# Mamba block and mixture of experts on one Trainium2 core: the last expert tiles in one run of pairs, begun on their own weights, with three partial sums in place of five

## The chip, the cores and the metric

The kernel runs on one core of a Trainium2 chip. The metric is the device time of one execution in microseconds. A core has TensorE (PE in the profile, its weight loads PEld), VectorE (DVE), ScalarE (ACT), GpSimd (POOL) and SyncE (SP, which here only issues transfers); each runs its own instructions in the order in which the program emits them and waits on semaphores. Sixteen DMA engines move the data that all queues ask for.

## What is computed

The input x has 4096 rows of 256 numbers, float32 throughout. Cut to what matters, with `ln` a layer norm over a row:

```python
# selective scan block (256 -> 512 inner channels, 16 states a channel)
x_in, z = split(x @ W_in.T)
u  = silu(causal_conv(x_in, 4 taps) + b_conv)
dt = softplus(u @ W_dt.T + b_dt);  B = u @ W_B.T;  C = u @ W_C.T
h[t] = exp(dt[t] * A) * h[t-1] + dt[t] * B[t] * u[t]      # per channel and state
y[t] = sum over states of h[t] * C[t]
x1 = ln(x + (y * silu(z)) @ W_out.T)
# mixture of 32 experts, 6 a row, and one shared expert
p = softmax(x1 @ router.T);  chosen = top6(p + bias);  w = p[chosen] / sum
out = ln(x1 + shared(x1) + sum over chosen e of w[e] * down[e](silu(gate[e](x1)) * up[e](x1)))
```

## The kernel before, in words

**Chunks and units.** The 4096 rows are cut into nine chunks: 256 rows, seven of 512, 256 (`SIZES`, NC = 9). The outer loop is the scan: 512 units, each one `tensor_tensor_scan` of 128 x 512 (L1236) on VectorE and one product with C (L1243). A full chunk has 64 units, the first and the last (numbers 0 and 8) have 32. Around a unit, `du_at` makes dt*u*B on POOL four units ahead (L1100), `exp_at` the decay on ACT two units ahead (L1111), `load_bc` fetches the broadcast rows of B and C by SP (bb and cb), and `summed` adds the product into PSUM by four TensorE transposes, three units late (L1157).

**Order by generators.** All else is written as Python generators in the list `threads`. `step()` advances each of them to its next `yield`; one such pass is called a round here. Nothing runs in Python on the chip: the rounds only set where each instruction stands in its engine's order. A unit of a full chunk emits one round, a unit of chunk 0 or 8 two, and behind the scan rounds follow without units. `rounds(k)` waits k rounds, `room()` waits for one of the PSUM banks (three while the scan runs, eight after it), `take` and `give` count live buffers.

**Beside chunk c** run `front(c + 1)` (projection, convolution, step sizes; its `gate(c)` makes z), `tail(c - 1)` (out-projection, norm, then `prepare`: router, top 6, places of the rows, shared expert), and tiles of chunk c - 2. With six units left, `drain(*mains)` steps until `front` and `tail` are through. `tail` adds the out-projection from PSUM to `row`, the chunk's rows of x (L1040; `row` has one buffer), two rounds after its matmuls (L1031). `prepare` reads the router's logits from PSUM one round after their matmuls (L317, L323). It starts `copies`, which scatters each row to its six places in `xs` by indirect DMAs of POOL, one a round (L553; `apart_from` asks that another POOL operation lies between two of them), and it writes the lists of rows and experts to DRAM (`order`). At its end it stores x1 plus the shared expert's part into the first partial sum, `acc[0]` (`base`, one buffer, L402 and L406).

**Tiles.** The scattered rows fill 224 tiles of 128 rows with one expert each, handled in 112 pairs. `loaded` issues a pair's transfers by SP: its rows (xt, L611) and weights of rows (wt, L613) and, for a tile with weights of its own, the expert's gu (256 KB, L622) and dn (128 KB, L627). `tiles` walks the pairs: it loads pair i, then begins pair i - `AHEAD`, with `gap` rounds between two begun. `pair` transposes the rows (L638, copied by ACT at L641), multiplies by gu (L679), applies the gate on ACT (tanh, L687) and VectorE (L690), multiplies by dn (L697) and scales on ACT (L655); `added` then adds each tile's 128 rows to a partial sum in DRAM by an accumulating indirect DMA of POOL (L661). `pair_of` does the same on the **wall**, a tile of all 32 experts' weights that stays in SBUF (L1285, tanh L1292, L1294 and L1295, transposes L1301, L1311).

**The wall's place** is that of the scan's operands: `cut` lays taps, W_dt, scratch, the inputs of the convolution, u, dt, the transposed x, W_in, z and W_out into it one after another, and `READY` notes up to which expert a place is free at four moments: at the start of chunk 8 (18 experts), when z of chunk 8 is made (22), when the scan is over (27), when the last out-projection has been emitted (32). `walls` issues the experts' loads in that order (L796, L800), one in three rounds while the scan runs.

**The end.** Tiles of chunks 1 to 6 (62 pairs) run on weights of their own beside the scan, into `acc[0]` to `acc[2]`. Then the program steps until the last out-projection and those tiles are emitted, and only then do the remaining 50 pairs (12 of chunk 7, 38 of chunk 8) begin, all on the wall, after `stored`, into `acc[2]` to `acc[4]`. Beside them `halfway` adds up `acc[0]` and `acc[1]` in SBUF (L1327 to L1330). When all is emitted, `finish` runs eight times on 512 rows: three loads of 512 KB (L1338), an add on POOL (L1340), two on VectorE (L1342, L1344), the norm (L179 to L193) and the store (L1347). A chunk's tiles can be loaded when its copies are all emitted (`copied`).

## Time and profile before

| what | value |
|---|---|
| runs of the kernel before | median 1891.46 us of 3 (1890.25 to 1893.32) |
| the profiled execution, its own time | 1901.56 us |
| its span, first to last instruction | 1899.9 us |
| busy in the span: PE, DVE, ACT, POOL | 72%, 75%, 56%, 64% |
| first scan L1236, last scan | 50.3 us, 1581.9 us |
| starts of the chunks 1 to 8 | 156, 323, 493, 669, 857, 1051, 1245, 1432 us |
| first wall group L1285, last | 1608.4 us, 1818.5 us |
| last accumulating DMA of POOL issued | 1835.15 us |

A row of the profile gives an operation with its line, its count, and the mean time of one. A window row gives each engine's busy time in a stretch with the number of instructions, the clock that TensorE was granted, the share of time that the DMA engines were busy, and GB/s. A row of waits says what an engine's instruction stood waiting for: total, times, longest. "issue" stands for time in which an engine waited for nothing that the profile shows.

### The profile page before, as it was taken

What the parts mean: (1) busy time and instruction counts of PE and PEld (TensorE: products, weight loads), DVE (VectorE), ACT (ScalarE), POOL (GpSimd) and SP (SyncE); (2) the same over time, 40 slices, a digit from 0 to 9 for tenths busy, and PEclk for the clock granted to TensorE, in tenths of its full rate; (3) what the DMA queues carried; (4) which work ended last, traced back from release to release, by engine and by line L of the source; (5) the groups of instructions that cost most, each with busy time, mean ns of one, the idle gap of its engine ahead of it and who ended that gap; (6) DMA issues with size and microseconds to landing.
All of it is one profiled execution on the core that took longest, in us unless ns stands there. A gap on an engine that the chain in (4) does not pass through costs nothing. (4 is left out here: it accounts for less than half of the span.)

```text
span 1899.9 us, 24943 instructions
## 1 busy us (share of the span) xinstructions
PE 1359.1 (72%) x6354; PEld 969.4 (51%) x6354; DVE 1430.4 (75%) x2435; ACT 1057.2 (56%) x2400; POOL 1220.2 (64%) x961
## 2 busy tenths in 40 slices
PE   6768665965786597868877896778766665799930
PEld 5335343633553365555556564666554544677720
DVE  2579899899889988997889788989986744233227
ACT  5586464555465456655666475647556442355523
POOL 1335555457556746895689667966895674677763
PEclk8777785987789689978988898789887787899965
DMA  8228975535744686988778887878878997699977
GB/s 247 80 83 285 277 227 169 158 97 164 226 133 116 173 241 195 220 206 238 209 201 216 225 229 182 220 218 247 210 192 228 276 257 193 113 202 210 168 150 264
DMA packets 349359, 377.22 MB, mean 199 GB/s; under 512 B 66816, under 2 KB 284480, under 8 KB 349216
## 3 DMA queue, kind: packets, MB, share of 16 engines
q1 hardware_dynamic: 305632, 317.78, 58.2%
q0 software_dynamic: 41472, 57.80, 16.1%
q8 instruction: 52, 0.85, 0.2%
q14 instruction: 91, 0.75, 0.1%
q10 hardware_dynamic: 2112, 0.05, 0.1%
HBM read 258.08 MB, written 117.43 MB: 198 GB/s over the span
## 5 line engine op out<-in xcount | busy, mean ns | idle before, releaser
L1100 POOL TENSOR_TENSOR du<-wall,bb 128x512 f32<-128x512 f32 x512 | 698.9, 1420 | 423.1 <-DVE h L1236 237.8
L1236 DVE TENSOR_TENSOR_SCAN h<-h,hlast,du 128x512 f32<-128x512 f32 x512 | 657.0, 1283 | 35.4 <-ACT h L1128 21.4
L1157 PE MATMUL y<-ident,hc 128*128 128x128 f32 x2048 | 362.5, 316 | 158.2 <-DVE hc L1243 148.8
L1157 PEld LDWEIGHTS y<-ident,hc 128*128 128x128 f32 x2048 | 282.2, 164 | 261.6 <-DVE hc L1243 194.6
L1243 DVE TENSOR_TENSOR hc<-h,cb 128x512 f32<-128x512 f32 x512 | 354.1, 692 | 59.7 <-DMA cb<-bcd 22.1
L1111 ACT ACTIVATE h<-wall,aneg 128x512 f32<-128x512 f32 (+1 forms) x576 | 371.0, 644 | 40.0 <-DVE hc L1243 21.5
L553 POOL DMA_INDIRECT xs<-row,at x192 | 192.3, 1002 | 95.2 <-DVE at L476 33.5
L661 POOL DMA_INDIRECT acc<-yt,no x124 | 196.8, 1587 | 66.3 <-ACT yt L655 31.5
L1138 ACT COPY hlast<-h 128x1 f32<-128x1 f32 x448 | 70.8, 158 | 256.4 <-DVE hc L1243 253.2
L661 POOL DMA_INDIRECT acc<-ytl,no x100 | 157.0, 1570 | 52.0 <-ACT ytl L655 19.9
L930 PE MATMUL pd<-wall 128*128 128x512 f32 (+1 forms) x288 | 127.4, 590 | 48.4 <-DVE hm L691 42.2
L679 PE MATMUL pg<-xsT,gu 128*128 128x128 f32 x992 | 135.3, 295 | 14.3 <-ACT hlast L1138 12.1
L679 PEld LDWEIGHTS pg<-xsT,gu 128*128 128x128 f32 x992 | 132.1, 211 | 21.5 <-ACT hlast L1138 12.8
L894 PE MATMUL pv<-wall 128*128 128x512 f32 (+1 forms) x288 | 120.5, 563 | 2.6 <-ACT hlast L1136 1.6
L697 PE MATMUL po<-dn,hm 128*128 128x256 f32 x248 | 79.2, 449 | 54.0 <-issue 33.4
L930 PEld LDWEIGHTS pd<-wall 128*128 128x128 f32 x288 | 57.2, 207 | 101.9 <-issue 90.8
L1285 PE MATMUL pg<-wall,xsT 128*128 x400 | 101.5, 400 | 0.0
L1294 DVE SCALAR_TENSOR_TENSOR gt<-gt,pg 128x256 f32<-128x256 f32 x50 | 21.0, 420 | 106.2 <-ACT gt L1292 82.4
L638 PE MATMUL pt<-ident,xt 128*128 128x128 f32 x448 | 72.6, 284 | 39.2 <-issue 18.3
L697 PEld LDWEIGHTS po<-dn,hm 128*128 128x128 f32 x248 | 50.5, 220 | 76.8 <-issue 41.3
L638 PEld LDWEIGHTS pt<-ident,xt 128*128 128x128 f32 x448 | 55.9, 146 | 63.2 <-issue 38.2
L641 ACT COPY xsT<-pt 128x512 f32<-128x512 f32 x112 | 65.5, 584 | 36.6 <-PE pt L638 28.4
(198 smaller groups left out, 2042.4 us busy)
## 6 DMA issues: line engine op xcount, KB each, us to landing
bb<-bcd SPq DMA_DIRECT2D x256, 256.0 KB
cb<-bcd SPq DMA_DIRECT2D x256, 256.0 KB
xs<-blank SPq DMA_DIRECT2D x55, 578.0 KB
gu<-in_gate_up_t_dram SPq DMA_DIRECT2D x124, 256.0 KB
xt<-xs SPq DMA_DIRECT2D x224, 128.5 KB
acc<-blank SPq DMA_DIRECT2D x32, 512.0 KB
dn<-in_down_t_dram SPq DMA_DIRECT2D x124, 128.0 KB
wall<-acc SPq DMA_DIRECT2D x24, 512.0 KB
```

The lines of the kernel that those rows point to most:

```text
L553: i = nc.gpsimd.indirect_dma_start(out=xs, out_offset=bass.IndirectOffsetOnAxis(ap=at[:, b, k : k + 1], axis=0), in_=row[:, b, :], in_offs ...
L638: nc.tensor.transpose(pt4[:, i, k, :], xt[:, i, ts(k, P)], ident)
L661: a = nc.gpsimd.indirect_dma_start(out=acc[lane + (j + i) % TURN], out_offset=bass.IndirectOffsetOnAxis(ap=no[:, i : i + 1], axis=0), in_= ...
L679: nc.tensor.matmul(pg[:, h, i, :], gu[i][:, k, ts(h, P)], xT[:, i, k, :], start=(k == 0), stop=(k == KD - 1),)
L697: nc.tensor.matmul(po[:, i, :], hm[:, i, :], dn[i], start=True, stop=True)
L894: nc.tensor.matmul(pv, taps[:, m, k, :], xin[:, m, k : k + Tc], start=(k == 0), stop=(k == TAPS - 1),)
L930: nc.tensor.matmul(pd, w_dt[:, k, ts(m, P)], u[:, k, :], start=(k == 0), stop=(k == M - 1),)
L1100: nc.gpsimd.tensor_mul(parts(q, du), u, row_for(q, 0))
L1111: nc.scalar.activation(h[:, ts(i, Tc)], dt_of[c][:, m + i, :], AF.Exp, scale=aneg[:, m + i, n : n + 1],)
L1157: nc.tensor.matmul(y_of[c, g][b // 2][:, b % 2, ts(m + j - 2 * g, P)], hc[:, ts(j * nb + b, P)], ident, start=(opens and j == 0 and b % 2 ...
L1236: nc.vector.tensor_tensor_scan(h, h, du_of.pop(q), hlast[:, n, m : m + 1], ALU.mult, ALU.add)
L1243: nc.vector.tensor_mul(parts(q, hc), parts(q, h), row_for(q, 1))
```

## The change

The tiles of chunks 6, 7 and 8 become one list, walked by one `tiles` from the start of chunk 8 to the end: 12 pairs of chunk 6 and the first 12 tiles (`EARLY`, six pairs) of chunk 7 on weights of their own, the other 44 pairs on the wall once it is stored. The program no longer steps until the earlier tiles are emitted; the scan's pools are closed right after its last product. Pairs on their own weights are begun one load behind (`AHEAD` 1 in place of 2), pairs on the wall two as before; a pair's load waits until three rounds after the matmuls on the buffer that it takes. u and dt of chunk 8, which are half as long, take the half of their places that lies next to the other, and z the second half of its place, so that other experts are free at the four moments (19, 5, 4 and 4 in that order). All tiles add into three partial sums; `halfway` and its sums are gone. The rows of chunk 8 have a tile of their own, loaded before the scan. `tail` waits three rounds in place of two before it reads PSUM (but not for chunk 8), `prepare` two in place of one. In chunk 8 only `last_gate` is drained. The copies of chunk 7 no longer wait for another POOL operation in between.

```diff
-    LANES = 5
-    TURN = 3
-    AHEAD = 2
+    LANES = 3
+    AHEAD = 1, 2
+    EARLY = 12
...
     def step():
+        clock[0] += 1
         threads[:] = [g for g in threads if alive(g)]
...
# prepare, between the router's matmuls and the maximum
         yield
+        yield
         mx = stat.tile([P, NB], F32, tag="mx", name=f"mx_{c}")[:, :nb]
...
# copies
-                while apart_from[0] and c < NC - 1:
+                while apart_from[0] and c < NC - 2:
                     yield
...
# added
-                out=acc[lane + (j + i) % TURN],
+                out=acc[(j + i) % LANES],
...
# pair, behind the matmuls on gu
         give("xsT")
+        used_at[j] = clock[0]
...
-    def tiles(items, gap, weights, one):
+    def tiles(items):
         st, going, begun = {}, [], [0]
+        def gap():
+            return 3 if scanned else 4
         def begin(upto):
             while begun[0] < upto:
                 k = begun[0]
                 begun[0] += 1
+                one = pair if items[k][2] else pair_of[0]
                 going.append(one(items[k][1], *st.pop(k)))
                 threads.append(going[-1])
-                yield from rounds(gap)
+                yield from rounds(gap())
-        for i, (c, j) in enumerate(items):
+        for i, (c, j, own) in enumerate(items):
+            weights = qw if own else None
+            ahead = AHEAD[not own]
+            if not own and not stored:
+                yield from begin(i)
+                while not stored:
+                    yield
             if c not in copied:
                 yield from begin(i)
                 while c not in copied:
                     yield
                 if c >= NC - 2:
                     yield from rounds(4)
             if weights is not None:
                 yield from take("dn", 4)
+                while i > 2 and clock[0] < used_at.get(items[i - 3][1], clock[0]) + 3:
+                    yield
             while i > 2 and items[i - 3][1] not in turned_out:
                 yield
             st[i] = loaded(c, j, weights)
-            yield from begin(i + 1 - AHEAD)
+            yield from begin(i + 1 - ahead)
...
# the places in the wall: cut(shape, moments at which its equal parts come free)
-    us[odd], dts[odd] = cut(M, T), cut(M, T)
-    z_all = cut(NB, DI)
+    us[odd], dts[odd] = cut((M, T), 0, 2), cut((M, T), 2, 0)
+    w_in = cut((KD, 2 * DI), 1)
+    xTs[odd] = cut((KD, T), 1)
+    z_all = cut((NB, DI), 1, 3)
+    w_out = cut((M, D), 3)
...
# walls: experts sorted by the latest moment that any part of their place needs
+        for e in sorted(range(E), key=lambda e: stages[e]):
+            while not free_at[stages[e]]():
+                yield
...
# front and gate, chunk 8
-            u = us[c % 2][:, :, :Tc]
+            u = us[c % 2][:, :, :Tc] if c < NC - 1 else half_of(us[c % 2], 1)
-            dt = dts[c % 2][:, :, :Tc]
+            dt = dts[c % 2][:, :, :Tc] if c < NC - 1 else half_of(dts[c % 2], 0)
-            z = z_all[:, : blocks(c)]
+            z = z_all[:, : blocks(c)] if c < NC - 1 else z_all[:, NB - blocks(c) :]
...
# tail
-                yield
-                yield
+                yield from rounds(3 if c < NC - 1 else 2)
                 part = row[:, 2 * h : 2 * h + 2, :D]
...
# before the scan
+        row_of[NC - 1] = const.tile([P, blocks(NC - 1), RW], F32, tag="row_last", name="row_last")
+        load_rows(NC - 1)
...
# in the scan
                 if 2 <= c:
-                    late = tiles(stage(c - 2), 4, qw, pair)
-                    threads.append(late)
+                    items = stage(c - 2)
+                    if c == NC - 1:
+                        items += stage(c - 1, 0, EARLY) + stage(c - 1, EARLY, own=False)
+                        items += stage(c, own=False)
+                    rest = tiles(items)
+                    threads.append(rest)
...
             if left[c] == 6:
-                drain(*mains)
+                drain(*mains[c == NC - 1 :])
...
# behind the scan
         last_tail = tail(NC - 1)
         threads.append(last_tail)
-        while NC - 1 not in z_done or late in threads:
-            step()
...
# finish
-        for i in range(TURN):
-            nc.sync.dma_start(part[:, i], rows_of(acc[LANES - TURN + i], b, MANY))
+        for i in range(LANES):
+            nc.sync.dma_start(part[:, i], rows_of(acc[i], b, MANY))
         yield
         nc.gpsimd.tensor_add(part[:, 0], part[:, 0], part[:, 1])
-        whole = sums[:, b : b + MANY, :]
-        nc.vector.tensor_add(whole, whole, part[:, 2])
         yield
-        nc.vector.tensor_add(whole, whole, part[:, 0])
+        whole = part[:, 0]
+        nc.vector.tensor_add(whole, whole, part[:, 2])
```

## The prediction

> **What bounds the kernel now.** I read the table of windows first, cut at the scan's chunks (the starts of L1236) and at what follows its end.
>
> ```profile
> core 0: us, PE busy (x) PEld busy (x) DVE busy (x) ACT busy (x) POOL busy (x), PEclk, DMA share, GB/s
> ...
> 1245.00:1432.00 187.00, 137.16 (x762) 112.26 (x762) 164.75 (x273) 108.51 (x256) 143.56 (x115) 0.84 0.82 219
> 1432.00:1583.00 151.00, 97.59 (x534) 79.92 (x534) 97.24 (x190) 76.56 (x205) 96.84 (x77) 0.79 0.95 254
> 1583.00:1605.00 22.00, 10.15 (x40) 7.91 (x40) 7.29 (x32) 6.13 (x11) 6.10 (x5) 0.66 0.75 212
> 1605.00:1640.00 35.00, 22.34 (x88) 17.52 (x88) 11.25 (x56) 6.94 (x19) 18.83 (x23) 0.74 0.61 115
> 1640.00:1820.00 180.00, 164.74 (x836) 131.60 (x836) 51.17 (x113) 99.84 (x278) 136.67 (x87) 0.97 0.91 175
> 1820.00:1840.00 20.00, 1.57 (x6) 0.88 (x6) 0.18 (x1) 3.22 (x6) 13.96 (x10) 0.59 0.64 84
> 1840.00:1900.00 60.00, 0.00 (x0) 0.00 (x0) 43.37 (x104) 18.13 (x40) 20.71 (x8) 0.50 0.84 274
> ```
>
> Six stages with six limits. A full chunk of the scan (row one) is VectorE's: 165 of 187 us. The last chunk (1432 to 1583) is not: its 32 units take 4.7 us each, where a scan and its product are 1.28 + 0.69; no engine is above two thirds, but the DMA share is 0.95. Then comes a hole of 22 us, in which the last out-projection and ten experts' weights are fetched; a slow start of 35 us; 180 us in which TensorE and POOL are both nearly full; 20 us of POOL alone; 60 us of VectorE and DMA. Next the waits in the last chunk and the timeline of POOL at the end of the tiles:
>
> ```profile
> DVE gt L690 <- ACT gt L687: 21.1, 6, 7.0
> ...
> DVE base L402 <- DMA acc<-base: 12.3, 1, 12.3
> ...
> DVE row L1040 <- DMA row<-in_x_dram: 9.6, 1, 9.6
> ```
> ```profile
> 1829.60 1.54 POOL L661 DMA_INDIRECT acc<-ytl,no  x1 [0.31 <-issue]
> 1831.45 1.55 POOL L661 DMA_INDIRECT acc<-ytl,no  x1 [0.30 <-issue]
> 1833.30 1.55 POOL L661 DMA_INDIRECT acc<-ytl,no  x1 [0.30 <-issue]
> ```
>
> The last chunk's scan stands behind tile products whose weights have not come (first row). And POOL's adds follow each other every 1.855 us, so a pair of tiles costs POOL 3.71 us; TensorE's cost for a wall pair is 3.62 us (starts of its group L1285 in the steady part: 1653.27, 1656.88, 1660.50). From 1654 on 92 adds take 183 us, of which 171 are this step and 12 are gaps: **POOL's queue, not TensorE, sets the end of the tiles**, at 1835.15 + 1.55 and 2.4 of landing, 1839.
>
> **The change, part by part**, against the profiled execution: span 1899.9, its own time 1901.56, 10.1 above the median 1891.46 of the runs. I sum in span and take 8.4 off at the end (1899.9 - 1891.46).
>
> *Chunks 0 to 7.* Lanes fall from 5 to 3: 16 fewer blanking stores of 512 KB in the second chunk, whose window has 14 us of idle VectorE in 167, 7 of it put to any wait and none of that to a DMA. I take 0 (bounds -5 and 0). Two more rounds in tail (L1040) and one in prepare (L323) put VectorE's read of PSUM behind one more unit. What VectorE waited for at L1040, and then at L323 (us, times):
>
> ```profile
>   DMA row<-in_x_dram: 17.5, 2
>   PE px L1031: 13.0, 5
> ```
> ```profile
>   PE pr L317: 15.6, 9
> ```
>
> 13.0 us at L1040, and 15.6 - 4.3 (the last, at 1600.8, is after the scan) = 11.3 at L323: 24 us of waiting that sits between scans on the bounding engine. The chain behind tail gets 3 rounds longer, 51 to 54 by my count, under the 58 after which it is drained. Bounds -24 and 0; I take -10, since a stall that goes often lets the next one show (hc waits for cb 22.1 us in all). AHEAD = 1: loads keep their rounds (one pair in four), pairs begin four rounds earlier. In chunks 4 to 6 the second xt of a pair (packets of 1028 B, the only ones of that size) landed 12 to 31 us before its transposes; four units earlier leaves 3 to 11 us, short only for the first two pairs of a chunk, by up to 5. TensorE runs some three units ahead of VectorE there (summed lags by three), which hides 5 us. Without that cover: 2 pairs x 5 us x 4 chunks = 40. In return SP no longer stands at L622 for gu (7.2 us in chunk 5). I take 0, bounds -15 and +40.
>
> *Chunk 8.* Here two rounds pass per unit and DMA is full: xt landed between 0 and 8 us before its use. Two units earlier, nine of the twelve pairs are short by 7 to 16 us. If DMA paces the scan, this only shifts the scan against SP by two units of 2 to 4.7 us: +4 to +9. Queued behind a transpose that waits are ACT's xsT copy and the exps, and so the scan. Two of the six new pairs are loaded and begun within the last two units (copied(7) is reached near round 56, four more rounds, and round 64 is the scan's end), without lead: one landing, 5 us, ahead of the last sums. The extra round takes 2 off the 9.6 at L1040. Excluding tail(7) from the drain gives nothing: its 51 rounds are over by then anyway, and the base wait of 12.3 stays. I take +7. **End of scan: 1583 - 10 + 7 = 1580.**
>
> *Scan end to the last add, now 256 us (1583 to 1839).* Row 8's load no longer waits for the copies of chunk 7 (SP's wait 13.3, VectorE's 7.8), eight or nine experts instead of ten wait for the end, and nothing waits for `late`. After the scan SP issues four pairs' loads (4.4 us a pair: 1546.41 to 1550.81) and some eleven experts (1.0 each: 1590.76 to 1591.76): 29 us, or 8.3 MB at the 255 to 342 GB/s of 1595 to 1605, 24 to 33. So the first wall pair starts 30 us after the scan, where it now starts 22.6 after (1605.64), but six pairs and most of the routing are done by then. Routing today costs the first wall pairs: five in 37 us where 19 would do. POOL's sum: 12 own adds x 1.855 = 22, 12 copies of chunk 8 x 1.29 = 15, 88 adds x 1.855 = 163: 201 us. Idle: 10 before its first own add; 4 ahead of pair 24, where copied(8) comes some four rounds late, since only six wall pairs now cover it; 8 of small gaps (12 now, part of them behind the halfway adds, 32.8 us of VectorE waits that go); 3.7 landing. **227 us.** TensorE's own sum, 44 x 3.62 + 30 + 13 of pipeline = 202, is less. The halfway loads and adds cost nothing more and give nothing by themselves: POOL is late next. If POOL's gaps vanish wholly: 213; if every hidden part shows (copies late by 12, start at 45): 250.
>
> The first wall groups of eight L1285 take 3.4 us in the chain, later ones 1.73; the granted clock is 0.50 in 1600 to 1605 and 1.00 in 1650 to 1655. An own pair costs 1.95 + 1.03 + 0.60 = 3.6 us of TensorE (groups L679, L697, L638); with all six at the half clock they cost 7.1 each, 43, and the wall starts near 45 instead of 30. I keep 30: SP's issue is the longer of the two at full clock, and the first own pair follows the scan's transposes without a pause.
>
> The Trainium skill, TensorE: Matmul & The Clock Gate, HAM oscillation, speaks against this part: after a gap of more than some 3.4 us each burst of matmuls starts at half clock, and own pairs that wait for their weights are such bursts. By the rule the start would be the 45 and the time 15 us longer, 1869; the rows bear it out for cold starts, not for this stream.
>
> *Finish, now 61 us.*
>
> ```profile
> 1879.08 2.35 POOL L1340 TENSOR_TENSOR wall<-wall 128x1024 f32<-128x1024 f32 x1 [3.15 <-DMA wall<-acc]
> ```
> ```profile
> 1886.44 1.22 DVE L1342 TENSOR_TENSOR sums<-sums,wall 128x1024 f32<-128x1024 f32 x1
> ...
> 1887.86 1.22 DVE L1344 TENSOR_TENSOR sums<-sums,wall 128x1024 f32<-128x1024 f32 x1
> ```
>
> One of two adds goes, 8 x 1.23 = 9.8 of VectorE's 43.4. But the three lanes' 12.6 MB load as before, until 1879.1; after that come 2.35 POOL, 1.22 and 2.4 VectorE: statistics end at 1885, not 1891.5. -6 (bounds -10 and 0). **55 us.**
>
> Sum: 1580 + 227 + 55 = 1862; less 8.4: **1854 us**, -2.0%.
>
> **Rivals.**
> 1. *Short lead (slower).* Own pairs wait for their weights in order on TensorE and the wait comes on top. Place: chunk 8's transposes L638. Price: six pairs already wait there today; if each loses its two units, 2 x 4.7 = 9.4, that is 56 less the 9 I took, plus half of the 20 to 40 in chunks 4 to 7. 1854 + 47 + 15 = 1916. It decides once the loss over all 68 own pairs passes 37 us, 0.55 a pair. For it: gt waits 21.1 us there already. Against it: the margins in chunks 4 to 6, and DMA as the pace. Chance 0.10.
> 2. *Hidden anyway.* Cold or starved own pairs fill the hole but start the wall late (45, not 30), and the waits at L1040 and L323 return elsewhere: 1854 + 15 + 7 = 1876. For it: DMA share 0.75 in the hole already. Chance 0.25.
> 3. *Full yield.* All 24 us of waits go, POOL's gaps too (213): 1854 - 14 - 14 = 1826. Chance 0.18.
> 4. *It doesn't do what it says:* chunk 7 is copied too late and no own pair runs before `stored`; then TensorE idles as now, 6 pairs are merely moved, and only the finish and the small rows gain: 22 for the six pairs behind the walls and 7 of the 18 that routing costs there, 1854 + 29 = 1883. Against it: 24 copies at one round each end near round 56. Chance 0.05.
>
> **How the numbers follow.** Forecast 1854, chance 0.42. A difference of 0.2% (3.8 us) is about what a measurement of this kernel tells from none. The range 1820 to 1890 takes in rivals 2, 3 and 4 and leaves out most of rival 1. Faster by over 0.2%: 0.86; within: 0.05; slower: 0.09, rival 1 but for its smallest sizes.
>
> **What would show it.** Right: the last L1236 at 1570 to 1590; own transposes after it and none of 15 us without TensorE; first wall group some 30 us behind; POOL's adds at 1.855 with under 10 us of gaps; one add of 128x1024 a step on VectorE in the finish, 4.2 us of work, and the loads as its limit. Wrong: PE pt <- DMA xt in tens of us, chunks 4 to 7 longer than 195 us, or adds waiting for lanes.

## The result, and the profile after

The changed kernel takes **1902.8 us** (median of 9 runs, 1899.1 to 1909.1), the kernel before 1894.2 (median of 9, 1890.3 to 1898.7): a ratio of 1.0048, 95% interval 1.0033 to 1.0062. It is half a per cent slower, where 2.0% faster was forecast; the time lies 49 us above the forecast and outside the range.

The profiled executions hide even that: the spans are 1899.9 before and 1901.1 after, since the profiled execution of before ran 7.3 us above its own median and that of after at its median. Stage by stage (starts of the scans, starts of the first and the last group of eight of the wall's matmuls, last add, all in us of the profiled spans; before's last group starts at 1817.0, and 1818.5 in the table of before is the start of a later matmul of that group; the last row counts to the end of the last store's issue):

| stage | before | after | after - before |
|---|---|---|---|
| chunks 0 to 3 (50.3 or 50.9 to the start of chunk 4) | 618.6 | 614.9 | -3.7 |
| chunks 4 to 7 | 763.1 | 780.2 | +17.1 |
| chunk 8, first to last scan | 150.0 | 146.4 | -3.6 |
| last scan to first wall group | 26.4 | 56.7 | +30.3 |
| first to last wall group (50 pairs, 44 pairs) | 208.6 | 178.3 | -30.3 |
| last wall group to last add issued | 18.2 | 15.4 | -2.8 |
| last add issued to the end | 61.2 | 54.7 | -6.5 |

The table of windows of the kernel after, cut as that of before was, from chunk 8 on (the columns are those of before):

```profile
1446.00:1593.80 147.80, 95.43 (x518) 79.01 (x518) 97.56 (x191) 77.62 (x206) 99.55 (x84) 0.80 0.96 255
1593.80:1645.00 51.20, 33.03 (x197) 29.05 (x198) 11.27 (x39) 16.04 (x39) 18.02 (x12) 0.80 0.93 250
1645.00:1693.00 48.00, 33.88 (x148) 27.61 (x148) 15.89 (x70) 15.41 (x42) 31.20 (x30) 0.82 0.67 108
1693.00:1832.00 139.00, 130.90 (x677) 104.61 (x676) 31.98 (x76) 80.99 (x224) 109.96 (x72) 0.99 0.86 139
1832.00:1850.00 18.00, 0.75 (x4) 0.32 (x2) 0.00 (x0) 2.12 (x3) 10.48 (x7) 0.58 0.69 117
1850.00:1901.00 51.00, 0.00 (x0) 0.00 (x0) 36.92 (x96) 18.13 (x40) 18.72 (x8) 0.50 0.93 309
```

The hole of 22 us is gone, but what took its place is two stretches, 99 us together, in which TensorE is busy for two thirds. Only from 1693 on does the wall run as forecast, TensorE at 131 of 139 us and a pair every 3.61 us. VectorE's waits in chunks 4 to 7 after the change (665.8 to 1446.0; total, times, longest):

```profile
DVE gt L696 <- ACT gt L693: 25.5, 13, 5.3
DVE h L1280 <- POOL du L1135: 18.7, 16, 2.3
DVE hc L1287 <- DMA cb<-bcd: 15.8, 5, 6.0
DVE gt L696 <- ACT hlast L1173: 14.4, 5, 5.3
```

The same view of before:

```profile
DVE hc L1243 <- DMA cb<-bcd: 21.9, 8, 6.4
DVE gt L690 <- ACT hlast L1138: 18.1, 8, 3.7
DVE h L1236 <- POOL du L1100: 8.5, 8, 2.3
DVE row L1040 <- PE px L1031: 6.8, 3, 2.4
DVE mx L323 <- PE pr L317: 6.2, 4, 1.9
DVE gt L690 <- ACT gt L687: 4.5, 2, 3.3
```

The two waits that the added rounds were to remove are indeed gone, row and mx, 13.0 us. But the wait of a pair's gate for ACT's tanh rose from 4.5 to 25.5 and the scan's wait for POOL's du from 8.5 to 18.7: 31 us against 13. Other waits fell, the one for cb by 6.1 and the gate's for hlast by 3.7, so that all waits of VectorE in these chunks together rose by 9.8 us, from 71.2 to 81.0. Most of the rest of the 17.1 is time in which VectorE is busy, 6.6 us more (665.43 and 672.07). The window row of before, then that of after:

```profile
668.90:1431.90 763.00, 594.67 (x3060) 444.92 (x3060) 665.43 (x1085) 454.49 (x1012) 567.47 (x448) 0.86 0.81 215
```
```profile
665.80:1446.00 780.20, 606.86 (x3060) 448.47 (x3060) 672.07 (x1085) 453.80 (x1011) 568.56 (x448) 0.86 0.79 210
```

Behind the scan, SyncE's queue (the timeline of after; start, duration):

```profile
1581.99 0.76 SPq L831 DMA_DIRECT2D wall<-in_down_t_dram  x1
1594.71 0.35 SPq L616 DMA_DIRECT2D xt<-xs  x1
```

POOL's queue at that time, the end of the scatters of chunk 7 among adds and du:

```profile
1587.52 0.99 POOL L558 DMA_INDIRECT xs<-row,at  x1 [0.30 <-issue]
1588.82 1.57 POOL L666 DMA_INDIRECT acc<-yt,no  x1 [0.30 <-issue]
1589.85 1.84 POOL L1135 TENSOR_TENSOR du<-wall,bb 128x512 f32<-128x512 f32 x1
1591.85 1.01 POOL L558 DMA_INDIRECT xs<-row,at  x1 [0.17 <-issue]
```

And what TensorE waited for in after, from the last scan to the first wall group:

```profile
PE pt L643 <- DMA xt<-xs: 28.5, 7, 16.2
PE pt L643 <- DMA dn<-in_down_t_dram: 2.2, 1, 2.2
```

The last scatter of chunk 7's rows starts on POOL at 1591.85. SyncE issues nothing for 12.0 us, until that scatter has landed at 1594.4, and only then asks for the first of the six new own pairs. All six are loaded behind the scan, one about every 7.4 us, and TensorE stands at their transposes for 28.5 us. In its order behind them stands the last tail. The routing of chunk 8 (`at`) and its scatters in before, by the view of that tile (durations in ns, first and last start):

```profile
L553 POOL DMA_INDIRECT xs<-row,at x12: 959/970/999, 1612.6 to 1638.2; - x12
L476 DVE TENSOR_SCALAR at<-best x1: 174/174/174, 1611.7 to 1611.7; 128x16 int32<-128x16 f32 x1
```

The same view of after:

```profile
L558 POOL DMA_INDIRECT xs<-row_last,at x12: 959/976/998, 1656.7 to 1684.2; - x12
...
L481 DVE TENSOR_SCALAR at<-best x1: 176/176/176, 1656.3 to 1656.3; 128x16 int32<-128x16 f32 x1
```

Routing is 45 us later, the last scatter 46; 10.5 us of that is the scan's own later end. So the wall, once begun at 1649.0, runs dry ahead of the first pair of chunk 8: between two wall groups, 1677.6 and 1692.0, lie 14.4 us, and SyncE issues nothing from 1660.7 to 1687.2. POOL's last adds in the timeline of after are 1.85 us apart, as before:

```profile
1840.91 1.54 POOL L666 DMA_INDIRECT acc<-ytl,no  x1 [0.30 <-DMA acc<-ytl,no]
1842.76 1.54 POOL L666 DMA_INDIRECT acc<-ytl,no  x1 [0.30 <-issue]
```

And in the finish VectorE has one add of 128x1024 a step where it had two (timeline of after, the last two steps):

```profile
1882.91 1.23 DVE L1372 TENSOR_TENSOR wall<-wall 128x1024 f32<-128x1024 f32 x1
...
1888.98 1.23 DVE L1372 TENSOR_TENSOR wall<-wall 128x1024 f32<-128x1024 f32 x1
```

### The profile page after: what moved, and what is told of

Same layout as the page of the kernel before. It is cut to its first block, busy times and chain, and to the rows that moved or that the text cites. A ratio compares the mean times of both kernels' runs of the same rounds, so it can differ in the third digit from the quotient of the medians.

```text
span 1901.1 us, 24918 instructions
## 1 busy us (share of the span) xinstructions
PE 1367.5 (72%) x6390; PEld 974.8 (51%) x6390; DVE 1423.4 (75%) x2411; ACT 1055.9 (56%) x2394; POOL 1216.2 (64%) x964
## 5 line engine op out<-in xcount | busy, mean ns | idle before, releaser
L1287 DVE TENSOR_TENSOR hc<-h,cb 128x512 f32<-128x512 f32 x512 | 354.1, 692 | 60.8 <-DMA cb<-bcd 17.4
L666 POOL DMA_INDIRECT acc<-yt,no x136 | 215.3, 1583 | 111.2 <-ACT yt L660 83.3
L558 POOL DMA_INDIRECT xs<-row,at x180 | 180.3, 1002 | 70.9 <-DVE at L481 30.7
L684 PE MATMUL pg<-xsT,gu 128*128 128x128 f32 x1088 | 154.5, 303 | 33.2 <-ACT hlast L1173 13.8
L684 PEld LDWEIGHTS pg<-xsT,gu 128*128 128x128 f32 x1088 | 151.1, 218 | 49.2 <-ACT hlast L1173 16.3
L666 POOL DMA_INDIRECT acc<-ytl,no x88 | 136.3, 1549 | 36.3 <-issue 12.1
L643 PE MATMUL pt<-ident,xt 128*128 128x128 f32 x448 | 76.9, 292 | 79.2 <-DMA xt<-xs 53.4
L1332 DVE SCALAR_TENSOR_TENSOR gt<-gt,pg 128x256 f32<-128x256 f32 x44 | 18.5, 421 | 131.4 <-ACT gt L1330 125.6
L696 DVE SCALAR_TENSOR_TENSOR gt<-gt,pg 128x256 f32<-128x256 f32 x68 | 28.4, 418 | 105.7 <-ACT gt L693 84.3
L1323 PE MATMUL pg<-wall,xsT 128*128 x352 | 87.6, 394 | 0.7 <-ACT xsT L646 0.7
```

Source lines behind the costliest of these rows:

```text
L558: i = nc.gpsimd.indirect_dma_start(out=xs, out_offset=bass.IndirectOffsetOnAxis(ap=at[:, b, k : k + 1], axis=0), in_=row[:, b, :], in_offs ...
L643: nc.tensor.transpose(pt4[:, i, k, :], xt[:, i, ts(k, P)], ident)
L666: a = nc.gpsimd.indirect_dma_start(out=acc[(j + i) % LANES], out_offset=bass.IndirectOffsetOnAxis(ap=no[:, i : i + 1], axis=0), in_=yt[:, ...
L684: nc.tensor.matmul(pg[:, h, i, :], gu[i][:, k, ts(h, P)], xT[:, i, k, :], start=(k == 0), stop=(k == KD - 1),)
L1287: nc.vector.tensor_mul(parts(q, hc), parts(q, h), row_for(q, 1))
L1323: nc.tensor.matmul(pg[:, i].rearrange("p h t -> p (h t)"), xT[:, i, k, :], w, start=(k == 0), stop=(k == KD - 1),)
```

## The experiments

Four suspects: the **lead** of one load for own pairs, the **added rounds** in tail and prepare, the **early own pairs** that stand ahead of the last tail, and, on the other side, the **three sums**, which should gain. All ratios are against the kernel before on the same chip, with 95% intervals in brackets; c4-7 is the time of chunks 4 to 7 and "wall" the time from the last scan to the first wall group, both from the one profiled execution of a run. One such execution says little about a few us: kernels whose program is alike in chunks 4 to 7 took 763, 767 and 770 us there (before, e4, e8), and 780, 786 and 784 (after, e2, e6).

| run | base | edit | ratio | c4-7 | last scan | wall |
|---|---|---|---|---|---|---|
| after | | | 1.0048 [1.0033, 1.0062] | 780 | 1592 | 57 |
| e1 | after | lead 2 | 0.9948 [0.9929, 0.9968] | 775 | 1581 | 59 |
| e2 | after | no early pairs | 0.9949 [0.9933, 0.9964] | 786 | 1597 | 20 |
| e3 | after | rounds back | 0.9981 [0.9967, 0.9995] | 772 | 1594 | 45 |
| e4 | before | three sums | 0.9896 [0.9875, 0.9916] | 767 | 1584 | 26 |
| e5 | after | lead 2, rounds back | 0.9848 [0.9825, 0.9870] | 753 | 1565 | 59 |
| e6 | after | early pairs held | 0.9994 [0.9980, 1.0009] | 784 | 1595 | 60 |
| e7 | before | lead 1 | 0.9991 [0.9977, 1.0004] | 770 | 1582 | 22 |
| e8 | before | three sums, row early | 0.9879 [0.9855, 0.9904] | 770 | 1591 | 21 |
| e9 | after | lead 2, prepare +1 | 0.9820 [0.9791, 0.9849] | 756 | 1569 | 62 |
| e10 | after | lead 2, prepare +4 | 0.9907 [0.9877, 0.9938] | 765 | 1573 | 68 |
| e11 | after | lead 2, tail +1 | 0.9780 [0.9752, 0.9809] | 749 | 1561 | 58 |
| e12 | after | lead 2, rounds back, no early pairs | 0.9807 [0.9769, 0.9845] | 751 | 1562 | 25 |
| e13 | after | lead 2, prepare +3 | 0.9934 [0.9919, 0.9948] | 777 | 1584 | 60 |
| e14 | after | lead 1, tail +1 | 1.0067 [1.0051, 1.0083] | 789 | 1607 | 52 |
| e15 | after | lead 1, prepare +1 | 0.9996 [0.9983, 1.0009] | 776 | 1595 | 43 |
| e16 | after | lead 2, tail +1, no early pairs | 0.9771 [0.9755, 0.9786] | 748 | 1559 | 22 |
| e17 | after | lead 1, four rounds later, rounds back | 0.9885 [0.9858, 0.9911] | 750 | 1576 | 48 |
| e18 | after | lead 1, four rounds later, tail +1 | 1.0049 [1.0028, 1.0070] | 780 | 1602 | 54 |

### Each suspect alone: e1 to e4

```diff
# e1: after with
-    AHEAD = 1, 2
+    AHEAD = 2, 2
# e2: after with
-    EARLY = 12
+    EARLY = 0
# e3: after with, in tail and in prepare
-                yield from rounds(3 if c < NC - 1 else 2)
+                yield from rounds(2)
-        yield
         yield
         mx = stat.tile([P, NB], F32, tag="mx", name=f"mx_{c}")[:, :nb]
# e4: before with LANES = 3, tiles added into acc[(j + i) % TURN], halfway and sums left out,
#     and in finish one add on VectorE, whole = part[:, 0] + part[:, 2]
```

> The changed kernel with AHEAD = 2, 2: pairs on their own weights are begun two loads behind again, all else as changed. Lead theory: chunks 4 to 7 (666 to 1446 us in the changed profile, 780 against 763 before) fall back to 763 +- 5, and the six pairs behind the scan wait less for xt (34 us of TensorE now): time 1875 to 1886. Rounds theory (the longer chain in tail and prepare costs the 17 us): chunks 4 to 7 stay at 780, time 1897 to 1903.

> The changed kernel with EARLY = 0: all 12 pairs of chunk 7 on the wall, 50 wall pairs. Start theory (the six own pairs are issued by SP at some 8 us each behind the scan and hold the wall back; then six wall pairs are too few to cover the copies of chunk 8, a hole of 14 us ahead of pair 24): first wall group some 20 us behind the scan instead of 57, no hole at pair 24, 50 x 3.62 = 181 us of pairs, time 1870 to 1882. Rival (the hole is filled either way, own pairs only move work): 1897 to 1905.

> The changed kernel with the two rounds in tail and the one in prepare before PSUM is read, as before the change. Rounds theory: chunks 4 to 7 fall from 780 to 763, time 1883 to 1888. Lead theory: chunks 4 to 7 stay at 780 or grow, chunks 1 and 2 lose the 5 us that they won (162.5 and 169.0 against 166.4 and 170.5), time 1903 to 1912.

> The kernel before with three partial sums for all tiles, no halfway sum, and the finish of the changed kernel; nothing else changed. If the finish's nine us (61 to 52) and the gaps of POOL and TensorE beside the halfway sums are due to this part alone: 1870 to 1880 against 1892. Rival (tiles behind the scan were paced by POOL anyway and the shared sums add waits): only the finish, 1881 to 1886, or less.

Each of the three suspects costs: the lead 1.0%, the early pairs 1.0%, the added rounds 0.7%. In chunks 4 to 7 neither e1 (775 us) nor e3 (772) comes back to the 763 that was expected of it. e2 started the wall 20 us behind the scan, as expected, but its 50 pairs took 201.8 us in place of the 181 expected, so its gain was smaller than that of the start. The three sums gain 1.0%: the wall's pairs take 191.3 us in place of 208.6, the finish 54.8 in place of 61.2. In e1 the wall starts as late as in after but runs without a hole, and TensorE hardly waits for rows (last scan to first wall group, 1581 to 1640):

```profile
PE pt L643 <- DMA xt<-xs: 3.9, 2, 3.5
```

### The lead in two other settings, and the early pairs held: e5 to e8

```diff
# e5: after with AHEAD = 2, 2 and e3's edits
# e6: after with, in begin, ahead of each pair of chunk 7
+                while items[k][0] == NC - 2 and NC - 1 not in z_done:
+                    yield
# e7: before, pairs on own weights begun one load behind (chunk 7's copies as in the change)
-            yield from begin(i + 1 - AHEAD)
-            if i < AHEAD:
+            ahead = AHEAD if weights is None else 1
+            yield from begin(i + 1 - ahead)
+            if i < ahead:
# e8: e4, and chunk 8's rows in a tile of their own, loaded before the scan
```

> The changed kernel with AHEAD = 2, 2 and the rounds before PSUM is read as before the change. If lead (ratio to the kernel before 0.9948 against 1.0048) and rounds (0.9981) are separate costs, they add: ratio 0.988, about 1872 where the kernel before has 1894, and chunks 4 to 7 take 763 to 767 us as before. If both cure the same wait, 0.993 to 0.996 and 770 to 775 us.

> The changed kernel in which the pairs of chunk 7 are not begun before the last out-projection is emitted; their loads keep their order. Queue theory (their transposes, which wait for rows, stand ahead of the last tail on TensorE, so the last routing and its copies come 45 us late and leave the hole of 14 us ahead of pair 24): last tail's transposes 4 to 8 us behind the scan instead of 19, routing 15 to 25 us earlier, no hole, time 1880 to 1890 against 1903. Rival (SP's 4.6 us a pair and 1 us an expert set the start alone): first wall group 57 us or more behind the scan as now, and whatever the hole gives is lost at the start: 1897 to 1906.

> The kernel before with pairs on their own weights begun one load behind instead of two, and chunk 7's copies free of the wait for another POOL operation, as in the changed kernel; nothing else. Lead theory: chunks 4 to 7 grow from 763 to 770 to 778 us, with gt waiting for ACT 20 us or more there instead of 4.5, time 1900 to 1906 against 1894. Rival (the lead is harmless by itself and costs only beside the six new pairs): 1891 to 1896.

> The kernel before with three partial sums and the short finish (ratio 0.9896), and the last chunk's rows in a place of their own, loaded ahead of the scan. SP stood 13 us for that row's buffer, ahead of the last ten experts. If that set the start of the wall pairs: they start 6 to 10 us earlier and the ratio is 0.985 to 0.987. Rival (the last experts wait for the out-projection anyway): at most 2 us, 0.989 to 0.990.

e5 gains 2.0% on after, at least e1's 1.0 and e3's 0.7 together (the 0.3 between them is within the intervals): with the rounds taken back, the lead alone (e3 to e5) is worth 1.3%. Only with both edits do chunks 4 to 7 fall to 753 us. e6 shows that the early pairs' place in TensorE's order made the hole: held behind the gate of chunk 8, the last tail's transposes stand 4 us behind the last scan and not 19, and the wall has no hole (161.3 us for 44 pairs); but the wall still starts 60 us late, because SyncE's queue is unchanged, so only half of the expected gain comes. e7 was a **miss** for the short lead: in the kernel before, a lead of one costs nothing that can be measured. e8 starts the wall 4 us earlier than e4, and its time can't be told from e4's.

### The added rounds one by one: e9 to e13

All have lead 2. In e9 and e11 one of the two edits of e3 is made, so that one added round stays; in e10 and e13 prepare has more:

```diff
# e10 (e13: 4 in place of 5), in prepare, with tail's round taken back
-        yield
-        yield
+        yield from rounds(5 if c < NC - 1 else 1)
# e12: e5 with EARLY = 0
```

> The changed kernel with AHEAD = 2, 2 and tail's rounds as before the change; only prepare's added round is kept (ratio without it 0.9848, with it and tail's rounds 0.9948). Length theory (each round more on the chain of tail and prepare costs alike; two of tail, one of prepare): a third of the 1.0%, ratio 0.988, chunks 4 to 7 at 760. Phase theory (what counts is where the routing's small VectorE operations fall within the four rounds of a pair): no such share; 0.985 or 0.995, whichever step of the pair it falls on.

> As e9_prep1, but with four rounds added in prepare (chunks 0 to 7), a whole pair's period. Phase theory: the routing falls on the same step of a pair as without any, ratio 0.984 to 0.988, chunks 4 to 7 at 753 to 760. Length theory: four rounds cost more than three, 0.995 to 0.999, chunks 4 to 7 at 775 or more.

> As e9_prep1 with the parts exchanged: tail's third round (twice a chunk) kept, prepare's taken back. Length theory: two thirds of the 1.0%, ratio 0.991 to 0.992. Phase theory: not two thirds; the sum of both parts need not come out.

> The changed kernel with AHEAD = 2, 2, the rounds as before the change and EARLY = 0 (all of chunk 7 on the wall). Start theory (a pair on its own weights costs SP 4.6 us in the hole behind the scan where a wall pair costs TensorE 3.6): first wall group 20 to 25 us behind the scan, six pairs more at 3.62, ratio 0.975 to 0.981. Rival (the hole has to be filled, and own pairs fill it): 0.985 to 0.990.

> The changed kernel with AHEAD = 2, 2, tail's rounds as before the change, and three rounds added in prepare: the routing behind the logits stands where both added parts of the change put it. Place theory (the routing three rounds later is what costs): as both parts together, 0.992 to 0.998, chunks 4 to 7 at 770 to 778. Pair theory (it is the two waits together, tail's later out-projection being part of it): 0.978 to 0.986, chunks 4 to 7 at 750 to 760.

The cost isn't the length of the chain: tail's round alone **gains** 0.7% on e5, prepare's alone costs nothing, both cost 1.0%, three in prepare cost 0.9% and four 0.6%. It goes by place. Of the theories, length failed in e11 and in e10; e13 came out as the place theory had it; e9's 0.9820 lies below both of its ranges, and e10's 0.9907 between its two, so the simple form by phase isn't right either. e12 shows that with lead 2 the early pairs gain nothing that can be measured (0.9807 without them, 0.9848 with them, the intervals overlap).

### The same at lead one, and the best version: e14 to e16

e14 and e15 are e11 and e9 with `AHEAD = 1, 2`; e16 is e11 with `EARLY = 0`.

> The changed kernel without prepare's added round, all else as changed (one line). If both parts together cost as they do at a lead of two: ratio 0.988 to 0.996 against 1.0048, chunks 4 to 7 at 765 to 772. If at a lead of one load the lead alone costs: 1.001 to 1.006, 778 or more.

> The changed kernel without tail's third round, prepare's round kept. Together-costs theory: 0.990 to 0.998. Lead theory: 1.001 to 1.006. Taking both out gave 0.9981.

> The changed kernel with AHEAD = 2, 2, without prepare's added round, and with EARLY = 0. If the gains of e11 (0.978) and of EARLY = 0 over EARLY = 12 (0.9807 against 0.9848) add: 0.972 to 0.976, first wall group 20 to 25 us behind the scan. Rival (the two measured on other chips differ by nothing): 0.977 to 0.981.

At lead one, tail's round, the best at lead two, is no better than after, whose interval its own overlaps: 1.0067 against 0.9780. e16 is the fastest kernel of the study, 1857.95 us and 2.3% under the kernel before, not to be told from e11.

### Is it the data or the place? e17 and e18

TensorE waited for a pair's rows in chunks 4 to 7 of after for 1.8 us in all, so late data could not be the price there. What the lead does to the order can be counted in the traces. How many of the chunk's scans stand ahead of a pair's gate (gt) in VectorE's order, with the same for the router's maximum (mx), in chunk 5:

```
kernel   lead  mx   scans ahead of the gates
before    2    20   13 17 21 25 29 33 38 42 46 50 53 57
e3        1    20    9 13 17 21 25 29 33 38 42 46 50 53
after     1    23    9 13 17 21 25 29 33 37 41 45 49 53
e5        2    20    1  5 13 18 23 28 33 39 45 51 56 61
e11       2    22    3  7 13 18 23 28 33 39 48 53 58 63
e1        2    23    2  6 13 18 23 28 33 38 45 52 57 62
```

So `AHEAD = 2` in the new program isn't what it was in the old: together with the new rule that a load waits for three rounds after the matmuls on its buffer, it spreads most of the twelve pairs five or six units apart over the whole chunk. (That it is this rule is read from the program; no run takes the rule out alone.) With lead one they stand four apart in the first 53 units. e17 and e18 keep lead one, and move the pairs to before's units; a pair's loads move with it:

```diff
# e17: e3 with, in tiles (e18: the same in e14)
+            if i == 0 and own:
+                yield from rounds(4)
             weights = qw if own else None
```

> The kernel after with the added rounds of tail and prepare taken back and AHEAD left at 1, 2, and four more rounds ahead of the first pair of each chunk's tiles: pairs are begun in the rounds of AHEAD 2, but their data are asked for in the same round, one load later than there. Landing theory (a pair begun at lead one works on data that come late): nothing is healed, chunks 4 to 7 stay at 772 us and the ratio at 0.995 to 1.000. Place theory (lead one only moves each pair four units earlier, onto other pieces of front and tail): chunks 4 to 7 return to 752 to 758, gt waits less than 6 us for ACT's gt there and TensorE's transposes of y wait for hc fewer than 10 times; the ratio is 0.985 to 0.990, with what chunk 8's late rows cost on top of 0.985.

> The same four rounds, with tail's third round kept and prepare's taken back (at AHEAD 1 this was 1.007, at AHEAD 2 0.978). Landing theory: 1.000 to 1.007, chunks 4 to 7 at 785 to 790. Place theory: 0.978 to 0.985, chunks 4 to 7 at 747 to 755, du and gt waits of VectorE there under 12 us together.

e17: with gates at 13 to 57, and data still asked for one load ahead, chunks 4 to 7 fall from 772 to 750 us, no longer than e5's 753. The waits show where, VectorE's in chunks 4 to 7, first in e3:

```profile
DVE gt L695 <- ACT gt L692: 20.9, 16, 3.3
DVE h L1279 <- POOL du L1134: 18.3, 14, 2.3
DVE hc L1286 <- DMA cb<-bcd: 12.5, 7, 3.3
```

The same view of e17:

```profile
DVE gt L695 <- ACT gt L692: 11.3, 9, 3.1
DVE h L1281 <- POOL du L1136: 11.0, 10, 2.3
...
DVE hc L1288 <- DMA cb<-bcd: 1.1, 3, 0.4
```

Two things fell, as far as rows can part them. The gate's wait and the scan's for du are 16.9 us shorter together: that is the pairs' place. The product's wait for cb is 11.4 us shorter: the pairs' loads, too, come four rounds later, and the scan's own rows come in time. e17 moves both at once. (Other waits grew by some 6 us.) The landing of the pairs' data isn't the price: TensorE waited for their rows for 1.3 us in e3 and for 0.7 in e17. e7 fits this: its gates stand in the units of e3's, and against before its wait for du is 12.4 us longer and its wait for cb 12.9 shorter, so that the short lead seemed free there. Two signs of the place theory did not come: gt still waits 11.3 us in e17, not under 6, and the transposes of y wait 20 times, not under 10.

In chunk 8 the landing may count: TensorE waits 28.6 us for rows in e17 there and not at all in e5, and the chunk takes 155.3 us, not 141.5. But it isn't the rows alone, since e11 waits for none there and takes 148.6, and after waits 17.3 us and takes 146.4. e17's last scan comes 11.6 us later than e5's, and its ratio is 0.4% higher. e18 is a **miss** for the simple form of the place theory: only 10 of the 40 us between e14 and e11 come back, and the ratio moves by 0.2%.

Where a chunk loses, by groups of units (counted from 0; mean of chunks 4 to 6, us, from the starts of the scans):

| units | before | after | e3 | e17 | e5 | e14 | e18 | e11 | e1 | e13 |
|---|---|---|---|---|---|---|---|---|---|---|
| 0 to 7 | 21.8 | 21.7 | 19.8 | 17.4 | 22.0 | 21.5 | 18.2 | 23.2 | 23.3 | 23.0 |
| 8 to 19 | 37.8 | 38.9 | 40.4 | 39.2 | 36.8 | 37.6 | 36.6 | 36.0 | 36.1 | 36.0 |
| 20 to 31 | 43.9 | 49.2 | 43.8 | 43.7 | 44.4 | 47.8 | 47.8 | 43.6 | 47.6 | 46.7 |
| 32 to 63 | 88.6 | 87.2 | 91.0 | 88.7 | 87.0 | 90.5 | 93.8 | 85.2 | 89.0 | 88.9 |

After loses 5.3 us a chunk in units 20 to 31, as much as its whole loss in these chunks (5.0 a chunk). The timeline of all engines shows how, first in before, chunk 6:

```profile
1121.44 0.37 DVE L348 TENSOR_TENSOR mask<-left,score 128x128 f32<-128x128 f32 x1
...
1122.97 1.91 ACT L906 ACTIVATE wall<-wall 128x2048 f32<-128x2048 f32 x1
...
1124.79 1.89 ACT L908 ACTIVATE wall<-wall 128x2048 f32<-128x2048 f32 x1
...
1126.59 0.36 ACT L687 ACTIVATE gt<-pg 128x256 f32<-128x256 f32 x1
...
1128.09 0.41 DVE L690 SCALAR_TENSOR_TENSOR gt<-gt,pg 128x256 f32<-128x256 f32 x1
```

and in after:

```profile
1131.06 1.91 ACT L936 ACTIVATE wall<-wall 128x2048 f32<-128x2048 f32 x1
...
1132.88 1.90 ACT L938 ACTIVATE wall<-wall 128x2048 f32<-128x2048 f32 x1
...
1134.68 0.82 ACT L660 ACTIVATE yt<-po,wt 128x256 f32<-128x256 f32 x2
...
1135.39 0.38 ACT L693 ACTIVATE gt<-pg 128x256 f32<-128x256 f32 x1
1135.41 1.58 POOL L666 DMA_INDIRECT acc<-yt,no  x1 [5.91 <-ACT yt L660]
...
1135.81 0.42 DVE L696 SCALAR_TENSOR_TENSOR gt<-gt,pg 128x256 f32<-128x256 f32 x1 [3.26 <-ACT gt L693]
...
1139.30 2.20 DVE L353 TENSOR_TENSOR mask<-left,score 128x128 f32<-128x128 f32 x1
1139.50 1.84 POOL L1135 TENSOR_TENSOR du<-wall,bb 128x512 f32<-128x512 f32 x1
```

In both kernels ACT's two passes of the softplus (3.8 us) stand ahead of a pair's tanh. In before, VectorE does the router's mask and sums (from 1121.44) while ACT is at it, and comes to the gate when the tanh is done. In after these stand three rounds later, **behind** the gate: VectorE waits 3.26 us at the gate and does them afterwards, with the scan in line behind both. POOL waits 5.91 us for yt at its add, and the next du with it. The router's block was the cover of ACT's softplus, and the added rounds took it away. The waits are 3.5 of the 5.3 us that after loses a chunk in these units; in before VectorE doesn't wait there at all.

The other 1.8 us are time in which VectorE is busy, and the rows show where most of it comes from: the mask took 0.37 us in before and 2.20 in after, where POOL's du runs beside it (the last row above) and the mask ends 0.16 us behind it. In chunks 4 to 7 of all twenty traces, 213 operations of VectorE took 0.7 us or more above the shortest of their kind, and every one of them ended 0.01 to 0.17 us behind the end of a du that ran beside it. So a block of small operations gets longer, too, where it meets more of these products.

The time of units 20 to 31 goes with the router's place: 43.7 to 44.9 us with 20 scans ahead of mx (before, e3, e4, e5, e7, e8, e12, e17), 46.7 to 49.2 with 23 (after, e1, e2, e6, e13). But the lost cover is the cause at lead one alone: VectorE waits 3.1 to 3.5 us a chunk there in after, e2 and e6, and not at all in e1 and e13, at lead two, where it is busy for longer. The windows of these units in chunk 6, of before, after and e1 (VectorE is busy for 41.45, 43.26 and 45.67 us in them):

```profile
1112.31:1156.06 43.75, 31.49 (x150) 20.01 (x149) 41.45 (x112) 24.44 (x49) 28.01 (x22) 0.88 0.69 185
```
```profile
1119.03:1168.49 49.46, 39.67 (x204) 27.93 (x202) 43.26 (x114) 29.66 (x61) 27.50 (x21) 0.90 0.64 170
```
```profile
1112.34:1160.44 48.10, 35.14 (x174) 23.05 (x172) 45.67 (x111) 27.18 (x54) 26.85 (x21) 0.90 0.62 164
```

With 21 or 22 scans ahead of mx it goes by the pairs: 44.7 and 46.2 in e9 and e15, 43.6 and 47.8 in e11 and e14, where the first of each has them spread. Which pair's instructions make that last difference was not traced, nor why units 32 to 63 cost 8.6 us more in e18 than in e11: that stays open. No run put the cover back alone, and none moved du away from the router's block: both causes are read from rows and from the runs' order, not tested one by one.

Over the eighteen runs and the two kernels the sum of the first two waits of after (gate for tanh, scan for du) goes with the time of chunks 4 to 7, at a correlation of 0.88: 5.5 us in e11 (749), 12.5 in e5 (753), 13.0 in before (763), 44.2 in after (780) and 55.1 in e14 (789). That goes with the time; it doesn't show the cause.

## Why the prediction was wrong, point by point

- **Where the 49 us lie.** In the prediction's own terms, the scan ends 14 us late (1593.7, not 1580), the stretch from there to the landing of the last add is 26 us longer (253, not 227, with the prediction's 1.55 and 2.4 behind the add's issue at 1842.76), and the finish is right. The other 10 us are 1.7 between span and time and the term "less 8.4": it took the excess of before's profiled execution over its median to hold for after's too, which ran at its median.
- **"I take 0" for AHEAD = 1 in chunks 4 to 7.** Failed, and for a reason that the step didn't hold. The margin of the loads was read rightly: transposes waited for rows for 1.8 us in all. But a pair begun four units earlier is another neighbour to everything else in order, ACT's softplus and POOL's du among it, and its loads meet others. The price depends on the rest: 5 to 11 us with the added rounds in (after, e2 and e6 against e1), 18 without them (e3 to e5), and 22 from e3 to e17, where the pairs and their loads move together; in the kernel before (e7) it could not be measured. The bound of +40 would have held it, by another mechanism (late weights).
- **"Two more rounds in tail ... I take -10."** Failed. The two waits went, as the step said (13.0 us in chunks 4 to 7). But the rounds moved the router's block past a pair's gate and beside other products of POOL, and what came was larger than what went: 8.5 us in all from e3 to after in these chunks, 22 from e5 to e1. "A stall that goes often lets the next one show" was written down and priced at nothing below zero; the bounds, -24 and 0, shut out what happened.
- **"Two of the six new pairs are loaded and begun within the last two units."** Failed: none was. The rounds were counted as order and taken for time: SyncE was through with all that stood ahead of the first of these loads at 1582.8, but POOL still had scatters of chunk 7 among its adds and du, and the last of them landed at 1594.4, 2 us after the start of the last scan.
- **"The first wall pair starts 30 us after the scan."** Failed. The prediction counts from the scan's end to the pair's transposes (22.6 before); that is 51 here (1593.7 to 1644.8), and 56.7 from the start of the last scan to the first group on the wall. SyncE starts 2.3 us behind the last scan, when those scatters have landed, and issues until 1639.4, 45 us in place of 29, of which two more pairs' loads are 8.8; the rows of the wall's first pairs come after that, and the first group 10 us later.
- **"4 ahead of pair 24."** Failed: 14.4. The last tail stood behind the early pairs' transposes in TensorE's order, so routing came 64 us behind the last scan, where it came 30 behind it before; e6 takes the hole away by that place alone.
- **End of scan, "1580".** The last scan starts at 1592.4 and ends at 1593.7: 17.1 lost in chunks 4 to 7, partly given back in chunks 0 to 3 and in chunk 8, which took 146.4, not 157.
- **Right:** the finish, forecast 55 and measured 54.7; the halfway adds, gone at no cost (e4); the wall's pace of 3.61 us a pair, with POOL at 1.85 an add. The three sums, with which two of these come, gain 1.0% by themselves (e4).
- **The rivals.** Nearest was the first, the short lead: pairs do stand in order, and it ends slower. Its place was wrong, chunk 8's transposes before the scan's end (17.3 us of waiting there, 9.0 before); its price fell behind the scan and, as a matter of place and not of late rows, in chunks 4 to 7. The third, that all waits go, is what e11 shows for the two waits at row and mx, which are gone there: with lead 2 and one added round the same program takes 0.978.
- **The clock.** The Trainium skill, TensorE: Matmul & The Clock Gate, HAM oscillation, let one expect bursts at half clock where matmuls wait for more than some 3.4 us in between. The stretch of the early pairs, 1593.8 to 1645.0, was granted 0.80, between the two; with hardly a wait for rows (1.0 us), in e11, the like stretch (1562.6 to 1618.8) was granted 0.88, and the wall started no earlier, 57.5 us behind the scan. Without early pairs, in e12, the stretch (1563.7 to 1587.5) was granted 0.82, and the wall started 25 us behind it. So the clock wasn't what made the start late.

## What to carry to other kernels

Before a block of instructions is moved by a few places, look at what it covers on the other engines: work of VectorE that lies between ACT's long pass and the user of ACT's next result is a cover, and moving it behind the user turns it into a wait. Look, too, at what then runs beside it: a block can get longer without waiting for anything. An option like a load's lead is tested in the program it is used in, since one new rule on buffers can turn it from a matter of data into one of spacing. Emitting work early in program order gains nothing if its inputs come from a queue that runs behind, and costs all that stands after it on its engine.

## What the runs showed of the hardware

- Single executions of the same program differ by more than many of the effects here: the profiled execution of before lies 7.3 us above the median of its runs, that of e7, 1889.7, lies 7.2 below (1896.9), and chunk 0, almost the same in all of these programs, took 103 to 107 us. So the stage tables say where time moves, and the ratios of the runs say how much.
- The loads at the start of a chunk go with a delay of the scan's own: the scan's product waits 21.9 us for cb in chunks 4 to 7 of before and 12.5 in e3, where the first pairs' loads are issued in the chunk's first rounds, and 1.1 us in e17 and 2.6 in e18, where they come four rounds later; units 0 to 7 fall from 21.8 and 19.8 us to 17.4 and 18.2.
- A small operation of VectorE can last as long as POOL's product beside it: the mask of 128x128 took 0.37 us in before and 2.20 in after, and all 213 such long operations ended 0.01 to 0.17 us behind a du. The scan of 128x512 keeps its 1.28 us beside a du (at 1136.60 in after, beside the one from 1136.44 to 1138.29).
